# Moving the joins of running sums behind an evacuation, a copy to ScalarE and a store to GpSimd, in a GroupNorm-attention kernel

## The chip, the cores and the metric

The kernel runs on one core of one Trainium2 chip. The metric is the device time of one execution in microseconds (us), the median of several runs; of the kernel before it is 1682.55 us (three runs, 1681.43 to 1687.45 us). One further execution was profiled; its span is 1681.9 us, and all times inside the kernel come from it. The engines are named as the profile names them: PE is TensorE (PEld its weight loads), DVE is VectorE, ACT is ScalarE, POOL is GpSimd, SP is SyncE, which in this kernel issues nearly all DMAs.

## The reference: what is computed

The input x has 4 images of 512 channels and 48 x 48 = 2304 positions. It is normalised in 32 groups of channels, projected to q, k and v, put through attention with 8 heads of 64 channels, projected back, and added to x:

```python
def _L0_conv_ref(x, gn_scale, gn_bias, qkv_w, qkv_b, proj_w, proj_b, num_heads):
    b, c, hh, ww = x.shape
    t = hh * ww
    d = c // num_heads
    hn = _group_norm(x, gn_scale, gn_bias)
    qkv = jnp.einsum('oc,bchw->bohw', qkv_w, hn) + qkv_b[None, :, None, None]
    qkv = qkv.reshape(b, 3, num_heads, d, t).astype(jnp.float16)
    q, k, v = (qkv[:, 0], qkv[:, 1], qkv[:, 2])
    scale = jnp.asarray(1.0 / math.sqrt(math.sqrt(d)), dtype=jnp.float16)
    w = jnp.einsum('bhct,bhcs->bhts', q * scale, k * scale)
    w = jax.nn.softmax(w, axis=-1)
    a = jnp.einsum('bhts,bhcs->bhct', w, v).astype(jnp.float32)
    a = a.reshape(b, c, hh, ww)
    out = jnp.einsum('oc,bchw->bohw', proj_w, a) + proj_b[None, :, None, None]
    return x + out
```

## The kernel before

Two heads make a pair `g` (16 pairs in all, 4 for each image). The queries of a pair are cut into blocks `j`: four of 512 and one of 256 positions, so there are 80 blocks. A block is worked off in bursts: six for a block of 512, three for a block of 256, so a pair has 27 bursts and the program 432. A burst is a step `n` of the main loop below. In it TensorE computes the scores of burst `n` (three tiles, each two heads by 512), ScalarE takes their exponential, VectorE adds the exponentials of burst `n - 1` to a running sum, TensorE multiplies the exponentials of burst `n - 2` with v, and one piece of side work (a chain of matmuls for the projection of q and k, of v, or of the output, with its evacuation from PSUM by VectorE) is issued by `fill`. Every engine works through its instructions in the order of the program, and the order is the one written here.

```python
    for n in range(end):
        now[0] = n
        while loads and loads[0][0] <= n:
            loads.popleft()[1]()
        # ... fetches ...
        summed = block_at(n - BEHIND - 1)      # BEHIND = 2: the block's last burst was n - 3
        pace(n)
        if summed:
            rows(*summed, add_up(*summed))     # sums over partitions, on PE; copied out by DVE
        wanted(stream[n][0])
        scores(stream[n])                      # PE, then exp on ACT
        if n > 0:
            add(stream[n - 1])                 # DVE
        if summed:
            fill(n)                            # a piece of side work: chain on PE, evacuation on DVE
        if n >= BEHIND:
            values(stream[n - BEHIND])         # PE
        if block_at(n - BEHIND - 2):
            check_sums(*block_at(n - BEHIND - 2))   # POOL
            invert(*block_at(n - BEHIND - 2))       # reciprocals, on DVE
        if block_at(n - BEHIND - 3):
            spread(*block_at(n - BEHIND - 3))       # DMA
        for late in (4, 5):
            found = block_at(n - BEHIND - late)
            if found and late == (4 if found[0] == NG - 1 else 5):
                divide(*found)                      # POOL
        if not summed:
            fill(n)
        # ... the last two blocks of the program ...
```

The running sum `acc` has three parts (one for each tile of a burst). After the block's last burst they are joined into one by two additions on VectorE, and `add_up` then sums over the partitions with a matmul against a matrix of ones:

```python
    def add(u):
        g, j, k, last = u
        pt = pts[u]
        if k == 0:
            acc[g, j] = [pt]                   # first burst of a block: no instruction
            return
        # ... the last blocks of the program ...
        t = acc[g, j][0]
        nc.vector.tensor_tensor(t, before, pt, ALU.add)
        if last:
            for r in range(1, BURST):          # BURST = 3: two joins
                nc.vector.tensor_tensor(t[:, 0], t[:, 0], t[:, r], ALU.add)
            acc[g, j] = [t[:, :1]]

    def add_up(g, j, bank=None, more=False):
        sl = ps_av.tile([P, QB], F32, tag="av", name=f"sl_{g}_{j}")   # shares the bank of av
        # ... for h in range(2):
                nc.tensor.matmul(sl[lo : lo + D, :n], ones16, t[:, r, h, a * n : (a + 1) * n], ...)
```

The bank `av` in PSUM exists once (`ps_av` has `bufs=1`): it holds the product with v of one block, is copied out, then holds the sums `sl`, is copied out again, and then takes the next block's product. The side work's bank `pw` also exists once (`ps_w`, `bufs=1`), so a chain starts only when the evacuation of the one before is done.

```python
        # values(u), after the block's last product:
        if last and u is not stream[-1]:
            avx[g, j] = work.tile([P, QB], F32, tag="avx", name=f"avx_{g}_{j}")
            nc.vector.tensor_copy(avx[g, j][:, :n], av[0][:, :n])

    def invert(g, j):
        # ...
        nc.vector.reciprocal(inv[:, :, :per], sums[g, j][:, :, :per])
        nc.sync.dma_start(row[:, :n].rearrange("h (p i) -> p h i", i=per), inv[:, :, :per])

    def divide(g, j):
        # ...
        nc.gpsimd.tensor_tensor(to, avx.pop((g, j))[:, :n], ibs.pop((g, j))[:, :n], ALU.mult)
        if g < NG - 1:
            # ... at: the place of this block in DRAM
            loads.append((now[0] + 1, lambda: nc.sync.dma_start(at, to)))
```

Of the kernel before, what the change touches and what calls it, by code (L numbers as in the profile page):

```python
# [17 lines left out]
ALU = mybir.AluOpType  # L18
# [11 lines left out]
NG = B * NPAIR  # L30
NT = T // P
SCALE = float(np.float16(1.0 / math.sqrt(math.sqrt(D))))
BURST = 3
BEHIND = 2
# [10 lines left out]
NQ = len(QBLOCKS)  # L45
# [422 lines left out]
def fast_path(  # L468
# [12 lines left out]
    nc = tc.nc  # L481
# [219 lines left out]
    qk, normed, now = {}, {}, [0]  # L701
# [114 lines left out]
    def prepare(upto, count):  # L816

        while pool_work and count > 0:
            k, which = pool_work[0]
            if k > upto or not there(k) or not free(k, which):  # L820
                return
            pool_work.popleft()
            if which == 0:
                weight_sums(wino[k][0])
            else:
                x_sums(k, which)
            count -= 1
# [180 lines left out]
    tasks, loads = deque(), deque()  # L1008
# [59 lines left out]
    def fetch(b, j):  # L1068

        o, n = QBLOCKS[j]  # L1070
        t = work.tile([P, NC, QB], F16, tag="attl", bufs=1, name=f"attl_{b}_{j}")
        pairs = NC - 1 if b == B - 1 else NC
        nc.sync.dma_start(
            t[:, :pairs, :n],
            atd[b].rearrange("(c p) t -> p c t", p=P)[:, :pairs, o : o + n],
        )
        fetched[b, j] = t
        fetch_at[b, j] = now[0]
# [87 lines left out]
    av, acc, pts, avx, sums, rowd, ibs = {}, {}, {}, {}, {}, {}, {}  # L1166

    stream = []
# [29 lines left out]
    def values(u):  # L1198
        g, j, k, last = u
        b, pr = divmod(g, NPAIR)  # L1200
        o, n = QBLOCKS[j]
        per = QB // n
        pt = pts.pop(u)
        if k == 0:
            if j == 0 and g == NG - 1:
                atts[g] = apool.tile([P, T], F16, tag="att", name=f"att_{g}")
            av[0] = ps_av.tile([P, QB], F32, tag="av", name=f"av_{g}_{j}")
        for r in range(BURST):
            for a in range(per):
                i = (k * BURST + r) * per + a  # L1210
                for h in range(2):
                    lo = h * D
                    nc.tensor.matmul(  # L1213
                        av[0][lo : lo + D, :n],
                        vv[b, pr // 2][:, i, pr % 2 * P + lo : pr % 2 * P + lo + D],
                        pt[:, r, h, a * n : (a + 1) * n],
                        start=(i == 0),
                        stop=(i == NT - 1),
                    )
        if last and u is not stream[-1]:  # L1220
            avx[g, j] = work.tile([P, QB], F32, tag="avx", name=f"avx_{g}_{j}")
            nc.vector.tensor_copy(avx[g, j][:, :n], av[0][:, :n])

    def add(u):

# [3 lines that stand above are left out]
            acc[g, j] = [pt]  # L1229
            return  # L1230
        if j >= NQ - 2 and g == NG - 1 and (last or j == NQ - 1):
            acc[g, j].append(pt)
            return
        before = acc[g, j][0]
        if k == 1:
            acc[g, j] = [
                work.tile(
                    [P, BURST, 2, QB], F16, tag="acc", bufs=1, name=f"acc_{g}_{j}"
                )
            ]  # L1240
        t = acc[g, j][0]
        nc.vector.tensor_tensor(t, before, pt, ALU.add)  # L1242
        if last:
            for r in range(1, BURST):
                nc.vector.tensor_tensor(t[:, 0], t[:, 0], t[:, r], ALU.add)  # L1245
            acc[g, j] = [t[:, :1]]

    def add_up(g, j, bank=None, more=False):
# [57 lines left out]
    def invert(g, j):  # L1306
        n = QBLOCKS[j][1]
        per = n // P
        inv = small.tile([P, 2, QB // P], F32, tag="inv", name=f"inv_{g}_{j}")
        nc.vector.reciprocal(inv[:, :, :per], sums[g, j][:, :, :per])  # L1310
        row = dram.tile([2, QB], F32, tag="row", name=f"row_{g}_{j}")
        nc.sync.dma_start(
            row[:, :n].rearrange("h (p i) -> p h i", i=per), inv[:, :, :per]
        )
        rowd[g, j] = row
# [11 lines left out]
    def divide(g, j):  # L1327
        o, n = QBLOCKS[j]
        b, pr = divmod(g, NPAIR)
        if g == NG - 1:  # L1330
            to = atts[g][:, o : o + n]
        else:
            to = work.tile([P, QB], F16, tag="att", name=f"att_{g}_{j}")[:, :n]
        nc.gpsimd.tensor_tensor(  # L1334
            to, avx.pop((g, j))[:, :n], ibs.pop((g, j))[:, :n], ALU.mult
        )
        if g < NG - 1:
            if b not in atd:
                atd[b] = dram.tile([C, T], F16, tag="attd", bufs=2, name=f"attd_{b}")
            at = atd[b][pr * P : (pr + 1) * P, o : o + n]  # L1340
            loads.append((now[0] + 1, lambda: nc.sync.dma_start(at, to)))


    beside = []
# [34 lines left out]
    def do_tasks(room):  # L1379
        while tasks and tasks[0][0] <= now[0] and room > 0:  # L1380
            _, us, run = tasks.popleft()
            run()
            room -= us
# [90 lines left out]
    for b in range(B):  # L1474
        g = b * NPAIR
# [102 lines left out]
    def issue():  # L1578
        us, run = beside.pop(0)[:2]
        run()  # L1580
        credit[0] -= us

    def pace(n):

        rate, work = 0.0, 0.0
        for p in beside:
            us, need = p[0], p[6]
            work += us
            left = min(need * per_pair, len(stream) - 4) - n
            rate = max(rate, work / max(left, 1))  # L1590
        credit[0] = min(credit[0] + rate, 4.0)

    def fill(n, tasks_too=True):

        idle = beside and beside[0][4] and not beside[0][4]()
        if ended(n - 1):
            room = 1.1 if idle else 0.0
        elif ended(n - BEHIND - 1):  # L1600
            room = 1.1 if idle else 0.5
        else:
            room = 2.4 if idle else 0.8
        if tasks_too:
            do_tasks(room)
        closed = False
        while beside:
            us, _, first, last, when, after = beside[0][:6]
            if after > n or (first and closed) or (when and not when()):
                break  # L1610
            if us > 0.1 and credit[0] < us / 2:
                break
            issue()
            closed = closed or last
        if tasks_too:

            turn = next((p[7] for p in beside if len(p) > 7), None)
            if turn is not None:
                prepare(turn + 1, 2)
# [11 lines left out]
    ended = lambda n: 0 <= n < len(stream) and stream[n][3]  # L1631
# [5 lines left out]
    def block_at(n):  # L1637

        return stream[n][:2] if ended(n) and n not in soon else None

    for n in range(end):
        now[0] = n
        while loads and loads[0][0] <= n:
            loads.popleft()[1]()
        while fetches and fetches[0][0] <= n:
            fetch(*fetches.pop(0)[1:])
        summed = block_at(n - BEHIND - 1)
        pace(n)
        if summed:
            rows(*summed, add_up(*summed))  # L1650
        wanted(stream[n][0])
        scores(stream[n])
        if n > 0:
            add(stream[n - 1])
# [4 lines that stand above are left out]
            values(stream[n - BEHIND])  # L1659
        if block_at(n - BEHIND - 2):  # L1660
            check_sums(*block_at(n - BEHIND - 2))
            invert(*block_at(n - BEHIND - 2))
        if block_at(n - BEHIND - 3):
            spread(*block_at(n - BEHIND - 3))

# [3 lines that stand above are left out]
                divide(*found)  # L1669
        if not summed:  # L1670
            fill(n)
        if n - BEHIND in soon:
            g, j = stream[n - BEHIND][:2]
            sx = rows(g, j, add_up(g, j))
            if n - BEHIND == soon[1]:
                divide_here(g, j, sx, avx[g, j], nc.gpsimd)
        if n - BEHIND - 1 == soon[0]:
            check_sums(g, j)
            invert(g, j)
        if n - BEHIND - 2 == soon[0]:  # L1680
            spread(g, j)
            divide(g, j)
    g, b, j = NG - 1, B - 1, NQ - 1
    n = QBLOCKS[j][1]
    values(stream[-2])
    while loads:
        loads.popleft()[1]()
# [3 lines left out]
    add_up(g, j, sl, more=True)  # L1691
    add(stream[-1])
    values(stream[-1])
    add_up(g, j, sl)

# [88 lines left out]
```

## Time and profile before: a small table

| what | value |
|---|---|
| time, median of 3 runs | 1682.55 us |
| span of the profiled execution | 1681.9 us |
| mean granted clock of TensorE | 0.988 |
| PE busy | 1567.4 us (93%) |
| ACT busy | 1306.3 us (78%) |
| DVE busy | 1302.0 us (77%) |
| POOL busy | 849.4 us (51%) |

The share of the span tells how much of the time an engine has work in hand; it does not tell what an engine waits for. The list of waits does: each of its lines names an instruction, what released it, the total of the waits in us, how many there were, and the longest. In a timeline a line begins with the start and the duration in us, then engine, line of the program, operation, and what is written from what; in square brackets stands the idle time of the engine before it and what ended that. The ends of matmuls are modelled, so the last matmul of a chain may overlap the next by 0.2 us.

### The profile page before, as it was taken

How to read it: one execution, taken by the hardware profiler on the slowest of the kernel's cores; microseconds unless marked ns; L12 is line 12 of the kernel's file. 1: busy time of each engine (PE TensorE's matmuls, PEld its weight loads, DVE VectorE, ACT ScalarE, POOL GpSimd, SP SyncE). 2: the span in 40 equal slices, each digit the busy share in tenths (PEclk: the TensorE clock that was granted, in tenths of full speed). 3: DMA queues.
4: the chain of work that ended last, by engine and by line, in shares of the span. 5: the costliest groups of instructions: out<-in, count | busy, mean ns of one | idle time of the engine just before them, and what ended most of it. 6: DMA issues, size and time to landing. Idle time of an engine off the chain costs nothing. (4 is left out here: it accounts for less than half of the span.)

```text
span 1681.9 us, 32495 instructions
## 1 busy us (share of the span) xinstructions
PE 1567.4 (93%) x12940; PEld 823.4 (49%) x12940; DVE 1302.0 (77%) x1632; ACT 1306.3 (78%) x1458; POOL 849.4 (51%) x962
## 2 busy tenths in 40 slices
PE   6998999899989999989999999998999999999997
PEld 2644545345444554545454454544545454545544
DVE  6288778877787778898787777888878877877665
ACT  3186776678888888878888878887888888888884
POOL 3076682645674573175567455505556844652111
PEclk9999999899999999999999999999999999999998
DMA  6002020000100015620101002352010010224524
GB/s 219 1 11 63 22 68 27 15 21 23 32 17 22 20 26 161 185 74 22 31 27 31 17 19 57 121 184 83 22 33 25 23 27 19 64 75 129 156 77 132
DMA packets 115637, 100.06 MB, mean 59 GB/s; under 512 B 52373, under 2 KB 81685, under 8 KB 115477
## 3 DMA queue, kind: packets, MB, share of 16 engines
q1 hardware_dynamic: 113444, 96.05, 20.2%
q8 instruction: 104, 1.70, 0.5%
q10 hardware_dynamic: 1904, 1.84, 0.4%
q14 instruction: 57, 0.46, 0.1%
q0 software_dynamic: 128, 0.01, 0.0%
HBM read 69.55 MB, written 28.01 MB: 58 GB/s over the span
## 5 line engine op out<-in xcount | busy, mean ns | idle before, releaser
L1195 ACT ACTIVATE p<-ps 128x1024 f16<-128x1024 f32 x1296 | 1231.7, 1028 | 338.0 <-PE ps L1188 286.9
L1242 DVE TENSOR_TENSOR acc<-acc,p 128x3072 f16<-128x3072 f16 x270 | 509.2, 1886 | 21.2 <-ACT p L1195 20.5
L1188 PE MATMUL ps<-q,k 64*128 64x512 f16 (+1 forms) x2880 | 363.8, 360 | 11.4 <-ACT p L1195 10.8
L1213 PE MATMUL av<-p,v 128*64 128x512 f16 (+1 forms) x2880 | 363.5, 365 | 3.6 <-DVE slx L1281 3.6
L797 POOL TENSOR_TENSOR t<-x,t 128x256 f32<-128x256 f32 x240 | 243.5, 1035 | 200.3 <-PE p L840 200.3
L1303 POOL TENSOR_SCALAR in<-sums 128x8 f32<-128x8 f32 (+1 forms) x158 | 103.8, 657 | 386.4 <-DMA sums<-slx 378.9
L988 PE MATMUL pv<-wqkv,x 128*64 128x256 f32 x2304 | 271.1, 382 | 16.6 <-DVE q L868 9.2
L1213 PEld LDWEIGHTS <-v 128*64 128x64 f16 x2880 | 133.9, 109 | 198.1 <-issue 151.1
L988 PEld LDWEIGHTS pv<-wqkv,x 128*64 128x64 f32 x2304 | 168.2, 137 | 107.1 <-issue 21.2
L1188 PEld LDWEIGHTS <-k 64*128 64x128 f16 x2880 | 108.1, 94 | 228.9 <-issue 181.8
L840 PE MATMUL p<-t,s 128*64 128x256 f32 x1440 | 181.0, 386 | 20.0 <-POOL t L797 6.1
L1334 POOL TENSOR_TENSOR att<-avx,ib 128x512 f16<-128x512 f32 (+1 forms) x78 | 114.2, 1464 | 124.1 <-DMA ib<-row 90.0
L797 POOL TENSOR_TENSOR t<-x 128x256 f32<-128x256 f32 x120 | 150.3, 1272 | 15.2 <-PE p L840 15.2
L1245 DVE TENSOR_TENSOR acc<-acc 128x1024 f16<-128x1024 f16 x156 | 146.0, 936 | 5.3
L840 PEld LDWEIGHTS p<-t,s 128*64 128x64 f32 x1440 | 102.7, 138 | 83.9 <-issue 13.0
L1242 DVE TENSOR_TENSOR acc<-p,p 128x3072 f16<-128x3072 f16 x79 | 142.4, 1803 | 0.0
L1092 PE MATMUL pr<-a,whi 128*128 128x512 f32 (+1 forms) x312 | 123.5, 403 | 11.5 <-ACT a L1064 4.3
L840 PE MATMUL p<-x,wqkv 128*64 128x256 f32 x960 | 115.7, 382 | 16.4 <-DVE k L868 12.0
L797 POOL TENSOR_TENSOR t<-x,x 128x256 f32<-128x256 f32 x120 | 126.5, 1073 | 0.0
L1092 PE MATMUL pr<-a,wlo 128*128 128x512 f32 (+1 forms) x312 | 115.5, 378 | 0.0
L996 DVE TENSOR_TENSOR v<-pv,bv 128x512 f16<-128x512 f32 x72 | 49.6, 689 | 82.2 <-PE pv L988 82.1
L840 PEld LDWEIGHTS p<-x,wqkv 128*64 128x64 f32 x960 | 69.6, 137 | 57.3 <-issue 13.0
(89 smaller groups left out, 1237.2 us busy)
## 6 DMA issues: line engine op xcount, KB each, us to landing
r<-x_dram SPq DMA_DIRECT2D x72, 256.0 KB, 3.2
out_dram<-r SPq DMA_DIRECT2D x69, 256.0 KB, 2.2
ib<-row SPq DMA_DIRECT2D x126, 128.0 KB, 3.0
x<-x_dram SPq DMA_DIRECT2D x62, 256.0 KB, 5.2
attd<-att SPq DMA_DIRECT2D x60, 128.0 KB, 1.7
attl<-attd SPq DMA_DIRECT2D x12, 512.0 KB, 4.3
x<-x_dram SPq DMA_DIRECT2D x16, 128.0 KB, 4.3
sums<-slx SPq DMA_DIRECT2D x128, 2.0 KB, 2.1
```

The costliest lines, as they stand in the source:

```text
L797: nc.gpsimd.tensor_tensor(t[:, c], ins[0][c], ins[1][c], ALU.subtract)
L840: nc.tensor.matmul(to[lo : lo + D, :], w[:, c, lo : lo + D], xs[c], start=(c == 0), stop=(c == 1),)
L988: nc.tensor.matmul(pw[0][lo : lo + D, a, :], hn[b, c, i * P // QB][:, at + lo : at + lo + D], wqkv[:, c, 2 * C + half * C // 2 :][:, : C / ...
L996: nc.vector.tensor_tensor(vv[b, half][:, i : i + 2, :], pw[0], bv[:, cols].unsqueeze(1).to_broadcast((P, 2, C // 2)), ALU.add,)
L1092: nc.tensor.matmul(ps[:, :n], w[:, c, bass.ts(m, P)], at32[b, j, c], start=(i == 0), stop=(i == len(steps) - 1),)
L1188: nc.tensor.matmul(ps[:, h, a * n : (a + 1) * n], kt[rows, bass.ts(i, P)], qt[rows, o : o + n], start=True, stop=True,)
L1195: nc.scalar.activation(pt[:, r], ps, AF.Exp)
L1213: nc.tensor.matmul(av[0][lo : lo + D, :n], vv[b, pr // 2][:, i, pr % 2 * P + lo : pr % 2 * P + lo + D], pt[:, r, h, a * n : (a + 1) * n], ...
L1242: nc.vector.tensor_tensor(t, before, pt, ALU.add)
L1245: nc.vector.tensor_tensor(t[:, 0], t[:, 0], t[:, r], ALU.add)
L1303: nc.gpsimd.tensor_scalar(t, sm, limit, None, op)
L1334: nc.gpsimd.tensor_tensor(to, avx.pop((g, j))[:, :n], ibs.pop((g, j))[:, :n], ALU.mult)
```

## The change

It has four parts. The two joins of a block leave `add` and are issued one in each of the two bursts after the block's last, each at the end of the step, behind `fill`; so an evacuation that follows in the same burst no longer stands behind them in VectorE's queue. The reciprocals of a block (`invert`) also move behind `fill`, for the same reason. The copy of the product with v out of its bank goes from VectorE to ScalarE. And the store of the finished block `att` to DRAM is issued by GpSimd directly behind its multiplication, where before SyncE issued it a burst later and held up its other DMAs until the multiplication was done. The last two blocks of the program (`joined` is false for them) keep their own way.

```diff
@@ values
         if last and u is not stream[-1]:
             avx[g, j] = work.tile([P, QB], F32, tag="avx", name=f"avx_{g}_{j}")
-            nc.vector.tensor_copy(avx[g, j][:, :n], av[0][:, :n])
+            nc.scalar.copy(avx[g, j][:, :n], av[0][:, :n])
@@ add
         nc.vector.tensor_tensor(t, before, pt, ALU.add)
-        if last:
-            for r in range(1, BURST):
-                nc.vector.tensor_tensor(t[:, 0], t[:, 0], t[:, r], ALU.add)
+
+    def join(g, j, r):
+
+        t = acc[g, j][0]
+        nc.vector.tensor_tensor(t[:, 0], t[:, 0], t[:, r], ALU.add)
+        if r == BURST - 1:
             acc[g, j] = [t[:, :1]]
@@ divide
-            loads.append((now[0] + 1, lambda: nc.sync.dma_start(at, to)))
+            nc.gpsimd.dma_start(at, to)
@@ main loop
+    def joined(n):
+        g, j = stream[n][:2]
+        return not (g == NG - 1 and j >= NQ - 2)
+
     for n in range(end):
@@ main loop, after values
         if block_at(n - BEHIND - 2):
             check_sums(*block_at(n - BEHIND - 2))
-            invert(*block_at(n - BEHIND - 2))
@@ main loop, after divide
         if not summed:
             fill(n)
+
+        if block_at(n - BEHIND - 2):
+            invert(*block_at(n - BEHIND - 2))
+        for r in range(1, BURST):
+            if ended(n - r) and joined(n - r):
+                join(*stream[n - r][:2], r)
```

## The prediction, made before the changed kernel was run

> **What bounds the kernel now.** I read the shares first, then the list of waits of PE, then a timeline of one block's end. The shares:
>
> ```profile
> PE 1567.4 (93%) x12940; PEld 823.4 (49%) x12940; DVE 1302.0 (77%) x1632; ACT 1306.3 (78%) x1458; POOL 849.4 (51%) x962
> ```
>
> PE is busy 93% of the span, so 1681.9 - 1567.4 = 114.5 us are idle. Part of that is the beginning: a table by stretches gives PE 27.67 us busy in the first 42.05 us, so 14.4 us are lost there, and 11.0 of the last 41.9 us. The change touches neither end much. In the middle (84.1 to 1640 us) PE is idle 1555.9 - 1467.4 = 88.5 us; that is the most the four parts together could win. Any new wait of PE, on the other hand, goes into the time nearly one for one, because nothing else is close to full. The list of waits, PE alone, says what the idle time hangs on:
>
> ```profile
> PE p L840 <- DVE k L868: 18.6, 19, 2.3
> ...
> PE pv L988 <- DVE q L868: 9.2, 11, 2.0
> PE p L840 <- POOL t L797: 6.1, 3, 3.4
> PE p L840 <- DVE q L868: 5.9, 10, 1.9
> PE p L840 <- DVE u3k L868: 5.6, 8, 0.9
> PE sl L1265 <- DVE avx L1222: 5.0, 6, 2.1
> PE p L840 <- DVE v L996: 4.7, 4, 2.8
> ...
> PE av L1213 <- DVE slx L1281: 3.6, 4, 2.4
> ```
>
> These are mostly one thing: a chain of side work (p, pv, pr) waits for the single bank `pw`, which DVE has still to evacuate (k, q, u3k, v). The rows of that kind add up to 57.7 us. The timeline of DVE and then of PE around one block's end shows where they come from:
>
> ```profile
> 870.10 1.42 DVE L1245 TENSOR_TENSOR acc<-acc 128x1024 f16<-128x1024 f16 x2
> 871.43 0.42 DVE L868 SCALAR_TENSOR_TENSOR u4q<-p,u2q 128x256 f32<-128x256 f32 x1
> 871.88 0.42 DVE L868 SCALAR_TENSOR_TENSOR q<-p,u4q 128x256 f16<-128x256 f32 x1
> 872.23 0.41 DVE L868 SCALAR_TENSOR_TENSOR k<-p,u3k 128x256 f16<-128x256 f32 x1
> 872.56 0.68 DVE L1222 COPY avx<-av 128x512 f32<-128x512 f32 x1
> 874.77 0.69 DVE L868 SCALAR_TENSOR_TENSOR k<-p,u3k 128x512 f16<-128x512 f32 x1 [1.53 <-PE p L840]
> 875.38 0.68 DVE L1281 COPY slx<-sl 128x512 f32<-128x512 f32 x1
> ```
>
> ```profile
> 872.78 1.95 PE L840 MATMUL p<-t,wqkv 128*64 128x256 f32 x16 [1.38 <-DVE k L868]
> 874.53 0.41 PE L1265 MATMUL sl<-acc,ones 128*64 128x512 f16 x2
> ```
>
> Call the block's last burst E. In burst E+1 DVE does the two joins (870.10, 1.42 us) and only then the three evacuations; the next chain, in burst E+2, starts at 872.78 when k is out, after 1.38 us of idle PE. That is the cost the change goes for. The second thing to see is at 874.53: the sums `sl` follow the chain of E+2 with no idle time at all, because the joins they read were finished three microseconds earlier, although the evacuation of that same chain (874.77) has not even begun.
>
> [...] the joins have one shape, yet run from 691 to 1652 ns with a median of 1096; for the sum below I take their mean, 0.94 us. [...] the trace has four small ones on POOL, of 542 to 782 ns.
>
> **The change, part by part.**
>
> *Joins, the gain.* I went through all 78 joined blocks and added the waits of PE that DVE ended, from the start of the joins to the start of `sl`: 43.8 us in 43 waits. A change of operand kind costs PE some 0.36 to 0.42 us of issue anyway (the timelines show it wherever nothing else waits), and a few of these waits would stay. I count a gain of **35 us**.
>
> *Joins, the cost.* In the new order the first join stands behind the evacuation of burst E+1 and the second behind the evacuation of burst E+2. `add_up` opens burst E+3 and reads `acc` after the second join. Between PE's end of the chain in E+2 and PE's `sl` nothing else is queued. So PE's path becomes: last matmul of the chain, evacuation on DVE, second join on DVE, then `sl`; all of what PE had after that (scores of E+3 and so on) stands behind it. The start of slx in the old trace is the moment at which DVE is free after that evacuation: 875.38 against 874.53 for `sl`, 0.85 us here. Going through all 79 places where `sl` opens a burst, 63 have an evacuation between; one of these is in the last blocks and keeps its way. The median of slx start minus `sl` start over them is 1.02 us (0.46 to 1.5, and one of 4.45 where weights were being split): three evacuations of 0.42 take longer than one of 0.69. Then the join, 0.94 us. So **62 x (1.02 + 0.94) = 122 us** of new idle PE. In the other 16 the burst has only the first half of a v chain or no chain, and the join is done in time.
>
> *Copy to ACT.* 79 copies leave DVE (50.1 us busy)[...]. It comes behind the three exponentials of E+2, and `sl` needs the bank. In the old trace the last exponential before `sl` ends between 3.6 us before and 0.8 us after the start of `sl`[...]. Where an evacuation stands between, the join is later still (1.96 us) and hides it; in the 16 others I count 16 x 0.2 = **3 us**. The 5.0 us of `sl` waiting for avx on DVE are in the 43.8 above where they fall there.
>
> *Reciprocals.* 14.9 us of DVE in 78 pieces, plus 8.4 us of idle DVE before them, no longer ahead of an evacuation; the rows leave up to a burst later, but the multiplication on POOL is three bursts further on. Some of POOL's 90.0 us of waiting for `ib` will grow. On PE: nothing to 3 us.
>
> *Store on POOL.* 75 issues leave SP, which stood 398.7 us before them, and put an estimated 75 x 0.6 = 45 us on POOL at 51%. PE waits for POOL only some 6 us (t) now. I count this, the reciprocals, and the waits elsewhere that shrink because the other engines catch up during the new ones, as **-5 us** together.
>
> Sum: 1682.5 - 35 + 122 + 3 - 5 = 1767.5, say **1768 us**, slower by 5%.
>
> **The rivals.** *First: the gain stands alone.* If the second join were done in time, the time would be 1682.5 - 35 - 5 = 1642 us, faster by 2.4%. For it speaks that burst E+2 adds nothing on DVE (its add belongs to the next block's first burst, which has no instruction), so DVE has room there, idle 1.53 us before the evacuation at 874.77. Against it: DVE works in order, so that room lies ahead of the evacuation and the join behind it, whatever the load. *Second: gain and cost cancel*, if the stall is half as long, say because the join runs at 0.69 us with POOL quiet, and other waits of PE shrink by 20 us or so while DVE and POOL catch up: 62 x (1.02 + 0.69) = 106, less 44 and 20, gives 1725 us. I give this little, because the 88.5 us of idle PE in the middle leave little more to win back. *Third: POOL becomes a bound* through the stores: its 849 us would have to grow by more than half; the waits of PE for t would have to rise from 6 to tens of us. Then 1790 us or more.
>
> **Range and chances.** The cost is a count of about 62 known from the trace times two durations that the trace has; I trust it to 15% (18 us). The gain lies between 25 and 60 us. Together this gives 1738 to 1792 us. Slower by over 2% means above 1716 us; to miss that the cost would have to fall below 75 us at the gain that I count. I give that 7%, and 3% to an oversight about the order that leaves the gain alone.
>
> **What would show it.** In the changed profile the list of waits must have a new row "PE sl <- DVE acc" with some 60 waits, 110 to 140 us in total and about 2 us each, and PE's share must fall to about 89%. The waits of p, pv and pr for DVE must fall from 57.7 us to about 20. DVE's queue must show evacuation, join, then slx, close together. ACT must be busy some 45 us more, DVE some 50 us less, POOL 40 to 80 us more. Were `sl` to wait instead for ACT's copy, or not at all, the step on the second join is wrong; were PE to wait for POOL's t by tens of us, the step on the store is.

## The result and the profile after

The changed kernel takes 1821.97 us (median of 4 runs, 1817.83 to 1824.22) against 1683.0 us of the kernel before: 1.0818 times as long, 95% interval 1.0789 to 1.0847. It is slower, as predicted, but by 139 us where the prediction has 85; the time lies outside the predicted range. The profiled execution spans 1822.5 us, 140.6 us more than before.

The engines' busy time, share of the span and instructions, from the page of the changed kernel:

```profile
PE 1603.8 (88%) x12940; PEld 823.4 (45%) x12940; DVE 1284.5 (70%) x1553; ACT 1341.7 (74%) x1537; POOL 828.1 (45%) x1037
```

ACT is busy 35.4 us more (45 were predicted, from an estimate that no trace had shown; the 79 copies take 44.9 us, part of it alongside the exponential before), DVE 17.5 us less (50 were predicted), and POOL 21.3 us less, where 40 to 80 more were predicted. PE's idle time is now 1822.5 - 1603.8 = 218.7 us, 104.2 us more than before. That leaves 36.4 us of the slowdown in PE's busy time, although PE executes the same 12940 matmuls. Two things are thus to be explained, not one. The list of PE's waits of the changed kernel (total us, number, longest):

```profile
PE sl L1268 <- DVE acc L1247: 141.9, 69, 6.7
PE ps L717 <- ACT x L675: 15.0, 2, 14.4
PE sl L1268 <- ACT avx L1222: 9.7, 10, 2.2
```

The predicted new row is there: `sl` waits for the join (acc, L1247), 69 times, 2.06 us each. The rows of p, pv, pr and pqk waiting for DVE (the waits for the side work's bank) add up to 19.7 us, against 60.3 before. So the idle time is told by its sum: 141.9 + 9.7 new, 5.0 of the old waits at `sl` and 40.6 of the waits for the bank gone, 106.0 against the measured 104.2.

What the prediction had not in it is the 6.7 us at the end of the first row. The timelines of PE, DVE and POOL at that place in the changed kernel, one after the other:

```profile
897.16 0.64 PE L1268 MATMUL sl<-acc,ones 128*64 128x512 f16 x2 [6.67 <-DVE acc L1247]
```

```profile
890.54 0.69 DVE L868 SCALAR_TENSOR_TENSOR k<-p,u3k 128x512 f16<-128x512 f32 x1 [1.52 <-PE p L840]
891.15 5.96 DVE L1247 TENSOR_TENSOR acc<-acc 128x1024 f16<-128x1024 f16 x1
897.84 0.69 DVE L1284 COPY slx<-sl 128x512 f32<-128x512 f32 x1 [0.73 <-PE sl L1268]
```

```profile
890.45 0.61 POOL L1344 DMA_DIRECT2D attd<-att  x1 [0.30 <-POOL att L1337]
891.08 1.41 POOL L797 TENSOR_TENSOR t<-x,t 128x256 f32<-128x256 f32 x2
892.44 1.40 POOL L797 TENSOR_TENSOR t<-x 128x256 f32<-128x256 f32 x2
893.80 1.39 POOL L797 TENSOR_TENSOR t<-x,x 128x256 f32<-128x256 f32 x2
895.16 1.39 POOL L797 TENSOR_TENSOR t<-x,t 128x256 f32<-128x256 f32 x2
```

The order evacuation (k), join, `sl`, slx is the one foreseen. But the join, whose median is 683 ns, takes 5.96 us. POOL has just issued the store (L1344) and then goes through eight subtractions with no idle time between them, 0.70 us each; the join ends 0.56 us after the last of them. Additions into the sum that take over 1.2 us longer than the shortest of their kind: none before, 20 after, each of them alongside such a closed row of POOL instructions behind a store; the 13 joins among them end 0.55 to 0.56 us after the last of the row, the 7 others 1.62 us. The longest addition of the kernel before, of 2.83 us where the median is 1.75:

```profile
1380.56 2.83 DVE L1242 TENSOR_TENSOR acc<-acc,p 128x3072 f16<-128x3072 f16 x1 [0.89 <-ACT p L1195]
```

The busy time of PE has to do with its clock. The mean granted clock fell from 0.988 to 0.965:

```profile
core 0: 1822.5 us, clock 0.965
```

The trace's record of the clock has it at half speed in 29 stretches (most of them 3.41 us long), against 8 before. PE was busy in 106.2 us of those stretches after and in 30.9 us before. In unbroken rows of seven or more, the matmuls of a chain for q and k (L840) follow one another there every 213 ns, elsewhere in the same trace every 108 ns (medians). So about half of PE's busy time in those stretches is lost: by my estimate from 106.2 and 30.9 us, 37.7 us more than before, close to the 36.4 us of added busy time.

### The profile page after: what moved, and what is told of

It is laid out like the page before. It is cut to its first block, busy times and chain, and to the rows that moved or that the text cites. A ratio compares the mean times of both kernels' runs of the same rounds, so it can differ in the third digit from the quotient of the medians.

```text
span 1822.5 us, 32530 instructions
## 1 busy us (share of the span) xinstructions
PE 1603.8 (88%) x12940; PEld 823.4 (45%) x12940; DVE 1284.5 (70%) x1553; ACT 1341.7 (74%) x1537; POOL 828.1 (45%) x1037
## 5 line engine op out<-in xcount | busy, mean ns | idle before, releaser
L1188 PE MATMUL ps<-q,k 64*128 64x512 f16 (+1 forms) x2880 | 372.7, 369 | 10.3 <-ACT p L1195 9.5
L797 POOL TENSOR_TENSOR t<-x,t 128x256 f32<-128x256 f32 x240 | 205.0, 875 | 224.2 <-PE p L840 223.6
L988 PE MATMUL pv<-wqkv,x 128*64 128x256 f32 x2304 | 279.2, 391 | 6.4 <-DVE k L727 4.5
L1306 POOL TENSOR_SCALAR in<-sums 128x8 f32<-128x8 f32 (+1 forms) x158 | 89.4, 566 | 400.3 <-DMA sums<-slx 393.0
L988 PEld LDWEIGHTS pv<-wqkv,x 128*64 128x64 f32 x2304 | 166.8, 141 | 104.7 <-issue 21.3
L840 PE MATMUL p<-t,s 128*64 128x256 f32 x1440 | 180.8, 388 | 3.5 <-DVE q L868 2.4
L1268 PE MATMUL sl<-acc,ones 128*64 128x512 f16 (+1 forms) x192 | 35.3, 393 | 151.6 <-DVE acc L1247 141.9
L1247 DVE TENSOR_TENSOR acc<-acc 128x1024 f16<-128x1024 f16 x156 | 163.2, 1046 | 0.7
L1242 DVE TENSOR_TENSOR acc<-p,p 128x3072 f16<-128x3072 f16 x79 | 150.0, 1899 | 0.0
L797 POOL TENSOR_TENSOR t<-x 128x256 f32<-128x256 f32 x120 | 130.4, 1107 | 22.6 <-PE p L840 22.4
L840 PEld LDWEIGHTS p<-t,s 128*64 128x64 f32 x1440 | 101.8, 140 | 66.9 <-issue 9.1
L797 POOL TENSOR_TENSOR t<-x,x 128x256 f32<-128x256 f32 x120 | 126.0, 1070 | 0.5 <-DVE x L668 0.4
L840 PE MATMUL p<-x,wqkv 128*64 128x256 f32 x960 | 121.7, 398 | 4.3 <-DVE v L996 2.8
```

Of the source, the lines that this page charges most:

```text
L797: nc.gpsimd.tensor_tensor(t[:, c], ins[0][c], ins[1][c], ALU.subtract)
L840: nc.tensor.matmul(to[lo : lo + D, :], w[:, c, lo : lo + D], xs[c], start=(c == 0), stop=(c == 1),)
L988: nc.tensor.matmul(pw[0][lo : lo + D, a, :], hn[b, c, i * P // QB][:, at + lo : at + lo + D], wqkv[:, c, 2 * C + half * C // 2 :][:, : C / ...
L1188: nc.tensor.matmul(ps[:, h, a * n : (a + 1) * n], kt[rows, bass.ts(i, P)], qt[rows, o : o + n], start=True, stop=True,)
L1306: nc.gpsimd.tensor_scalar(t, sm, limit, None, op)
```

## The experiments

My theory after the result had three parts: the second join behind the evacuation of burst E+2 is the main cost, as predicted; a DMA issued by POOL keeps VectorE's additions waiting; and the half clock follows from PE's new waits. The first rival (R1 below) was that the store is the main cost and the joins are cheap; the second (R2) that the joins are everything and the store is neutral. Each run is compared with runs of the kernel before on the same chip, so the ratio counts and not the bare time; where a ratio is turned into us below, it is by 1682.5 us.

| edit | ratio to before | 95% interval |
|---|---|---|
| the whole change | 1.0818 | 1.0789 to 1.0847 |
| store on POOL alone | 1.0162 | 1.0129 to 1.0195 |
| joins moved alone | 1.0412 | 1.0381 to 1.0443 |
| the change with the store back on SP | 1.0471 | 1.0431 to 1.0512 |
| joins split around the evacuation of E+2 | 0.9773 | 0.9747 to 0.9798 |
| copy on ACT alone | 1.0091 | 1.0074 to 1.0108 |
| reciprocals moved alone | 1.0057 | 1.0043 to 1.0070 |
| before, plus a DMA of 2 KB on POOL | 1.0178 | 1.0151 to 1.0205 |
| before, plus a memset on POOL | 1.0004 | 0.9992 to 1.0016 |
| joins moved, plus idle matmuls in the wait | 1.0393 | 1.0375 to 1.0411 |
| both joins behind the evacuation of E+1 | 0.9806 | 0.9787 to 0.9824 |
| the change with the second join ahead of the evacuation | 1.0268 | 1.0244 to 1.0293 |
| the same with the store back on SP | 0.9924 | 0.9910 to 0.9938 |

**Store on POOL alone.**

```diff
-            loads.append((now[0] + 1, lambda: nc.sync.dma_start(at, to)))
+            nc.gpsimd.dma_start(at, to)
```

> The kernel before with the store of att issued by POOL and nothing else changed. Theory A (the second join behind the evacuation of burst E+2 is the main cost; the lost clock follows from PE's stalls; the store adds a little because VectorE's additions of two SBUF operands are kept out while POOL runs on behind its DMA): some 10 to 20 additions on VectorE longer than 3 us, no new wait of PE for the joins, 1690 to 1705 us. Rival R1 (the store on POOL is the main cost): 1750 us or more. Rival R2 (the store is neutral): 1678 to 1686 us and no long additions.

Slower by 1.6%, some 1710 us, above the 1690 to 1705 us of theory A; R2 falls for the store, and R1 too, since that is a fifth of the slowdown. Seven VectorE instructions took over 1.3 us longer than the median of their kind (four additions of 4.8 to 7.2 us, a join of 3.7 us and two normalisations), fewer than I had put on record, and they are among what makes the evacuations late: the waits of side work for its bank rise from 60.3 to 70.8 us.

**Joins alone.** The edit is the change's own for `add`, `join` and the end of the step; the rest is as before.

> The kernel before with the two joins moved as in the change, and nothing else (reciprocals, copy and store as before). Theory A: PE waits some 70 times about 2 us for the second join, 130 to 140 us, wins back some 40 us of waits for the bank of side work, loses 20 to 35 us to half clock: 1785 to 1805 us, and no addition on VectorE over 3 us. R1: the joins cost what was predicted at most or less, 1720 us or less. R2: all of the slowdown, 1815 to 1825 us.

Slower by 4.1%, some 69 us, below what theory A had. The row that decides it, from PE's waits of this run:

```profile
PE sl L1268 <- DVE acc L1247: 122.7, 71, 5.4
```

That is the predicted 122 us almost to the number, which is partly luck (see the next section). The waits for the bank fall to 8.7 us, a gain of 51.6, not 35 us. R1, with 1720 us or less, is too low: the joins alone cost less than the prediction had for the whole, yet they are the largest part.

**The change with the store back on SP.**

```diff
-            nc.gpsimd.dma_start(at, to)
+            loads.append((now[0] + 1, lambda: nc.sync.dma_start(at, to)))
```

> The changed kernel with the store of att back on SP. Theory A: the long additions vanish (none over 3 us), the waits for the second join fall from 142 to some 125 us, 1790 to 1808 us. R1: most of the slowdown goes, 1725 us or less. R2: unchanged, 1817 to 1825 us.

No addition over 3 us is left, and the ratio falls from 1.0818 to 1.0471. The wait of `sl` for the join, from PE's waits of this run:

```profile
PE sl L1268 <- DVE acc L1247: 116.8, 65, 5.7
```

The two profiled executions differ by 52.1 us (1822.5 and 1770.4; the kernel before took 1683.0 and 1688.2 beside them). With the store on POOL, VectorE is busy 45.5 us longer with as many instructions (1284.5 against 1239.0), PE is idle 39.2 us longer, 25.1 of them in the row above, and by half of PE's busy time at half clock (106.2 against 79.0 us) the lower clock costs an estimated 13.6 us more. So behind the moved joins the store costs 3.5%, some 58 us, more than twice what it costs alone. The additions were foreseen by theory A; the time was foreseen by none of the three, R1 being too low, A and R2 too high.

**Joins split: the first behind the evacuation of E+1, the second ahead of the evacuation of E+2.** Against the whole change, this undoes one half of one part; here it stands on the kernel before, with `add` and `join` as in the change and this in the main loop:

```diff
+        if ended(n - 2) and joined(n - 2):
+            join(*stream[n - 2][:2], 2)
         if not summed:
             fill(n)
+        if ended(n - 1) and joined(n - 1):
+            join(*stream[n - 1][:2], 1)
```

> The kernel before with the joins spread over two bursts, the first behind the evacuation of burst E+1 as in the change, the second in burst E+2 AHEAD of the evacuation, so that it is done while PE is still at that burst's chain. Theory A: no wait of PE for the join, the waits for the bank of side work fall from some 60 to some 20 us, 1640 to 1660 us. If instead moving a join anywhere behind an evacuation costs, or the join ahead of the evacuation delays it as much as before: 1675 to 1700 us.

Faster than the kernel before by 2.3%, which was forecast; the wait of `sl` for the join is not quite gone, as the row further down shows. The timeline of DVE at one block's end of this run shows the order that does it:

```profile
852.92 0.68 DVE L1247 TENSOR_TENSOR acc<-acc 128x1024 f16<-128x1024 f16 x1
853.68 0.69 DVE L1222 COPY avx<-av 128x512 f32<-128x512 f32 x1
854.29 0.68 DVE L1247 TENSOR_TENSOR acc<-acc 128x1024 f16<-128x1024 f16 x1
855.13 0.69 DVE L868 SCALAR_TENSOR_TENSOR k<-p,u3k 128x512 f16<-128x512 f32 x1 [0.16 <-PE p L840]
855.74 0.68 DVE L1284 COPY slx<-sl 128x512 f32<-128x512 f32 x1
```

The second join (854.29) is done while DVE would have stood idle for the chain; the evacuation k still waits 0.16 us for PE behind it, so it is not held up; and slx follows it with no join between. From PE's waits of the same run:

```profile
PE sl L1268 <- DVE acc L1247: 11.3, 14, 3.6
```

The joins alone and this run differ only in the place of the second join: ahead of or behind one evacuation. That place is worth 4.1 + 2.3 = 6.4% of the time. PE's share is 95% here. No kernel run has a lower ratio, though the interval overlaps that of both joins behind the evacuation of E+1, further down.

**Copy on ACT alone.** The edit is the change's own line.

> The kernel before with only the copy of the product with v moved to ScalarE. Theory A: with the joins early, nothing hides the copy: it stands behind the three exponentials of burst E+2, so the sums wait for the bank in the half of the blocks whose last exponential ends late; a new row of PE waiting at sl for ACT's avx, 10 to 25 us, slower by 0.3 to 1.2%. Rival: 50 us less on VectorE let its evacuations come earlier: faster by 0.3% or more.

Slower by 0.9%. From PE's waits:

```profile
PE sl L1265 <- ACT avx L1222: 18.6, 29, 2.2
```

The 5.0 us that `sl` waited for VectorE's copy are gone, so this is 13.6 us more, and PE's idle time grows by 13.8 us (114.5 to 128.3). VectorE is busy 45.9 us less (1256.1 against 1302.0), and it brings nothing that shows: the bank's release now lies behind three exponentials on ACT, which in the trace of before have a median of 1.02 us each.

**Reciprocals alone.** The edit is the change's own move of `invert`.

> The kernel before with only the reciprocals moved behind fill. Theory A: within 0.4% of before; POOL waits longer for ib (120 to 200 us against 90), which PE does not feel. Rival: the later reciprocals push POOL's multiplication and with it the sums of x that PE reads: slower by 0.5% or more, PE waiting over 12 us for POOL's t.

Slower by 0.6%, about 10 us, which is outside theory A's 0.4% and inside the rival's range. POOL's wait for ib grows to 147.9 us, as theory A had it, but PE's wait for t is 7.4 us against 6.1, not the 12 of the rival, so the way in which the rival said it would cost is hardly seen. PE is idle 9.3 us longer (123.8 against 114.5): 2.9 us are waits for the bank, 3.2 are waits for POOL's t and s together, and the rest is scattered. Why they grow stays open.

**What is it about the store on POOL?** Two runs on top of the kernel before, whose store stays on SP:

```diff
+            junk = dram.tile([P, NC], F32, tag="junk", bufs=2, name=f"junk_{g}_{j}")
+            nc.gpsimd.dma_start(junk, gsc)
```

> The kernel before, its store still on SP, and in addition a DMA of 2 KB (128 x 4 floats to a scratch place in DRAM) issued by POOL behind each multiplication att. Theory A (a DMA instruction on POOL itself makes POOL run through what is queued behind it without giving VectorE's additions of two SBUF operands a turn): additions of 3 us and more appear as in the run with the store on POOL, five or more, and the time is slower by 1 to 2%. Rival (the cost is the transfer's data or the lost wait of SP): no long additions, within 0.5% of before.

```diff
+            junk = work.tile([P, QB], F16, tag="junk", bufs=1, name=f"junk_{g}_{j}")
+            nc.gpsimd.memset(junk, 0.0)
```

> The kernel before, its store still on SP, and in addition a memset of 128 x 512 fp16 on POOL behind each multiplication att[...]. Theory A: no addition over 3 us, within 0.7% of before. Rival (any instruction of POOL that reads nothing lets a run of POOL start that VectorE cannot break): long additions as with the DMA, slower by 1 to 2%.

The DMA of 2 KB costs 1.8%, as much as the store of up to 128 KB within the intervals; the memset, which keeps POOL busy 0.52 us each time, costs nothing. It is therefore neither the data, nor the time POOL spends, nor the order of SP: the store on POOL takes the transfer off SP, the small DMA leaves it there, and both cost the same, so freeing SP of its 398.7 us of waiting is worth nothing that these intervals would show. In the run with the small DMA 11 VectorE instructions were over 1.3 us longer than the median of their kind, in that with the memset none. The place of the longest, POOL and then DVE:

```profile
921.45 0.58 POOL L1343 DMA_DIRECT2D junk<-gsc  x1
922.06 1.42 POOL L797 TENSOR_TENSOR t<-x,x 128x256 f32<-128x256 f32 x2
923.43 1.41 POOL L797 TENSOR_TENSOR t<-x,t 128x256 f32<-128x256 f32 x2
924.80 1.40 POOL L797 TENSOR_TENSOR t<-x 128x256 f32<-128x256 f32 x2
926.16 1.40 POOL L797 TENSOR_TENSOR t<-x,x 128x256 f32<-128x256 f32 x2
927.53 1.39 POOL L797 TENSOR_TENSOR t<-x,t 128x256 f32<-128x256 f32 x2
```

```profile
923.70 6.84 DVE L1242 TENSOR_TENSOR acc<-p,p 128x3072 f16<-128x3072 f16 x1
930.47 0.47 DVE L727 TENSOR_SCALAR q<-pqk,bqkv 128x256 f16<-128x256 f32 x1
```

It is the same picture as in the changed kernel: DMA, a closed row of POOL, and a VectorE addition, here of 6.84 us, that ends 1.62 us after the row is over (928.92).

**Is the half clock a consequence of the waits?** To the joins alone, ten matmuls are added ahead of each `add_up` (the edit in part); they write into the bank that the burst's scores overwrite, and nobody reads them.

```diff
+            spun.append(ps_s.tile([P, 2, QB], F32, tag="ps", name=f"warm_{n}"))
+            for _ in range(5):
+                for h in range(2):
+                    part = slice(h * D, (h + 1) * D)
+                    nc.tensor.matmul(
+                        spun[0][:, h, :], kt[part, :P], qt[part, :QB], start=True, stop=True
+                    )
             rows(*summed, add_up(*summed))
```

> The run with the joins alone moved (4.1% slower than before), and in addition ten matmuls of scores ahead of every add_up, into the bank that the burst's own scores overwrite: work nobody reads, some 1.3 us, laid into PE's wait of about 2 us for the second join. Theory A on the clock (half-clock stretches follow PE's idle time in those waits): the stretches of half clock fall from 18 to about 8, and although PE does more, the time falls by 0.3 to 1.2% against the joins alone, to 1.029 to 1.038 of before. Rival (the clock falls for another reason, or its loss is not on the path): stretches unchanged, time equal or longer, 1.041 to 1.055.

The half-clock stretches fall from 18 to 6, and the mean clock rises from 0.979 to 0.992, while the waits of `sl` for the join shrink from 122.7 to 43.4 us. So in these two runs the waits do cause them. The time is 1.0393 against 1.0412, and the intervals overlap: that the run is faster is not shown, and my lower bound for the gain was too optimistic. The traces show why. From the end of the chain to `sl` PE needs 134.8 us in all with the added matmuls and 123.0 without, 11.8 us more, because they also run where there was little to wait for. Yet the span is 4.6 us shorter (the kernel before is 1.4 us faster on this chip), so some 16 us were gained elsewhere: PE's other matmuls are busy for 1563.3 us instead of 1581.8. PE's busy time inside half-clock stretches fell from 60.1 to 19.5 us; half of the difference, an estimate of what the clock gave back, is 20.3.

**Does the burst matter in which a join runs?** On the kernel before, with `add` and `join` as in the change, both joins at the end of burst E+1:

```diff
+        if ended(n - 1) and joined(n - 1):
+            for r in range(1, BURST):
+                join(*stream[n - 1][:2], r)
```

> The kernel before with both joins behind the evacuation of burst E+1, none in E+2. Theory A (only the order against the evacuations matters; the burst in which a join runs does not): no wait of the sums for the joins beyond a few us, the waits for the bank as low as with the joins split (24 us), 0.970 to 0.982 of before. Rival (two joins in a row hold up what follows on VectorE, the copies out of av and the evacuation of E+2): 0.985 to 1.0.

Faster by 1.9%, with no wait of `sl` for a join; 18.1 us of `sl` waiting for avx on VectorE take its place. Of burst and order, it is the order against the evacuation of E+2 that costs.

**Could the change be mended by that one line?** The changed kernel, with its second join moved ahead of the evacuation as in the split run.

> The changed kernel with one line moved: the second join ahead of the evacuation of burst E+2 instead of behind it; store on POOL, copy on ACT and reciprocals as in the change. Theory A (the parts add: joins split -2.3%, store +1.6, copy +0.9, reciprocals +0.6): 1.000 to 1.016 of before, so the change would not be faster even so. Rival (the other three parts were only harmful together with the late join): 0.985 or less.

It is slower by 2.7%, well above the 0.8% which the parts alone sum to. What I had on record, that the parts add, was wrong. The last run takes the store off POOL again:

> The run before it (the change with the second join ahead of the evacuation, 1.027 of before) with the store of att back on SP; copy on ACT and reciprocals stay moved. The parts alone sum to -2.3 + 0.9 + 0.6 = -0.8%. Theory A (the surplus of that run over the sum of its parts comes from POOL's DMA meeting the joins in their new places): no addition over 3 us, 0.985 to 0.997 of before. Rival (the copy and the reciprocals together with the split joins make the surplus): 1.003 to 1.015.

This is 0.9924, and -2.3 + 0.9 + 0.6 = -0.8%: the other parts do add, and the surplus is the store's. On POOL it costs 1.6% with the joins in their old place and 3.4 to 3.5% with either of the new ones. In the traces with the store on POOL and moved joins 14 (the change) and 13 (second join ahead) joins take over 1.7 us, with the joins in their old place 2. The joins now stand where POOL's closed rows are, and `sl` waits for them directly. From PE's waits with the second join ahead, the store on POOL and then on SP:

```profile
PE sl L1268 <- DVE acc L1247: 32.9, 16, 4.5
```

```profile
PE sl L1268 <- ACT avx L1222: 36.2, 66, 2.2
PE sl L1268 <- DVE acc L1247: 4.6, 3, 3.5
```

The 28.3 us between the two acc rows are most of the 38.1 us that PE is idle longer with the store on POOL (138.2 against 100.1). The avx row shows what is left to win in the last kernel: with the join early, the copy on ACT is what `sl` waits for.

## Why the prediction was wrong

**The step that failed is the store.** The prediction put "-5 us" on the store, the reciprocals and the waits that shrink, together, and asked only whether POOL would become a bound by its busy time (the third rival) or PE would wait for t. Neither happened: POOL's busy time fell to 828.1 us, PE's wait for t to 2.9 us. The store cost 27 us alone and 58 us on top of the moved joins, through an engine that the prediction did not have in view there: VectorE, held up by POOL. For the length of the joins it did have POOL in view. In the trace of before the 53 joins during which POOL executes nothing take 691 to 694 ns, and the other 103 have a median of 1099 ns (up to 1652). The prediction took the mean of all joins, and did not ask the same of the store. The issue on POOL is short, as it had been put (0.6 us, from the four DMAs that POOL issues in the trace of before, of 542 to 782 ns): the 75 issues of the change take 578 to 697 ns, though 64 of them overlap an addition. Not the DMA is held up, but the additions (20 of them by over 1.2 us), by what POOL executes behind it, and `sl` or an evacuation waits for them.

**The cost of the joins was right in its mechanism, and its number was lucky.** Predicted 62 x 1.96 = 122 us; with the joins alone, 122.7 us in 71 waits of 1.73. Two errors cancelled: 61 of the waits are where the prediction counted them, 103.9 us in all or 1.70 each, and ten, with 18.8 us, are in blocks that it held free. The join behind its new place has a median of 681 ns, not the 0.94 us taken from the old mean.

**The gain of the joins was too small.** Predicted 35 us, measured 51.6 with the joins alone and 40.6 in the change: with the joins out of the way nearly all waits for the bank go, including some that I had put down to other things. Of the 43.8 us counted, the prediction took off 8.8, because a change of operand kind would cost PE 0.36 to 0.42 us anyway. That was a misreading: in the trace of before 445 idle times of this size with no cause shown stand before weight loads (PEld) and none before PE's own matmuls, which follow within 0.15 us at 1277 of their 1369 changes of line.

**The clock was missing.** No term of the sum stood for it. By half of PE's added busy time in half-clock stretches, my estimate as above, it costs 37.7 us in the change, 24 us with the store back on SP ((79.0 - 30.9) / 2) and 14.6 us with the joins alone ((60.1 - 30.9) / 2).

**Copy and reciprocals.** I counted 3 us for the copy, 16 x 0.2, where no join hides it; the length of a copy on ACT was an estimate of mine that no trace had shown. On DVE before, the 79 copies have a median of 681 ns; on ACT in the change, the 64 of 512 columns have a median of 607 ns (597 to 651). In the change `sl` waits 9.7 us for it, in 10 places, seven of 0.5 us and three of about 2. Alone, with no late join to hide it anywhere, it costs 0.9%, 15 us. The reciprocals were put at 0 to 3 us of gain and cost 0.6% alone.

Without the store the change measures 1.0471, some 1762 us, and the prediction of 1768 would have held; but partly because two errors, the gain too small and the clock left out, cancelled. Of the rivals, the first (the second join done in time, a gain alone, 1642 us) was refuted for this order. With the join in time the joins by themselves do gain (1682.5 x 0.9773 = 1644 us), but the whole change does not: 1.0268, some 1728 us. Two slips in the sums change nothing: the 57.7 us of waits for the bank leave out rows below 0.7 us (59.3 with them, 60.3 with pqk), and the cost of the joins below which the change would not be slower by 2% is 71 us at the gain counted, not 75.

## What to carry to other kernels

In the timelines shown, VectorE works in the order of the program. Moving the joins "out of the way" behind an evacuation that waits for PE made their reader wait for that evacuation too (`sl`, 69 times, 2.06 us each): before moving, ask who reads the result next, and use an idle stretch ahead of the wait rather than the place behind it. A DMA of 0.6 us on GpSimd behind each multiplication cost 1.6 to 3.5% of the time here: judge such a DMA by what stands queued behind it, and look for VectorE's longest additions, not their median. The waits of PE cost twice here, once as idle time (104.2 us more in the change) and once as a lower clock (0.965 against 0.988), so compare the busy time of equal work as well.

## What the runs showed of the hardware that I had not expected

In the traces with a DMA issued by GpSimd behind each multiplication, its tensor operations run in closed rows behind that DMA (0.70 us each in the rows shown; in the kernel before, the subtractions of L797 have a median of 0.73 us but a mean of 1.10, since some take up to 2.33), and some VectorE additions into the running sum end only after the row: in the changed kernel 20 of them, up to 7.66 us for one whose median is 1.75 us. In the kernels without these DMAs the longest is under 2.9 us. With a memset beside the store on SP the longest is 2.82 us; with a DMA of 2 KB there it is 6.84 us. Why the DMA does this was not tried.

In these traces half clock follows waits of PE of about 1.9 us and more, though not all of them. Within a trace the half-clock stretches begin at whole multiples of 3.41 us from one another. Laid on that grid, the middle of the changed kernel's trace (100 to 1650 us) has 34 intervals in which PE was busy less than half; half clock follows on 28 of them, and once on another. With the joins alone it is 17 of 24, and none elsewhere; in the kernel before 6 of 10, and two elsewhere. In the changed kernel the longest wait inside those 28 intervals is never shorter than 1.88 us, but one of 1.93 was not followed by half clock; in the kernel before, one interval whose longest wait was 1.18 us was.
